# Recurrence of a state-space layer: ACT's and PE's side work moved between slots of a hand-written order

## The chip, the cores and the metric

One core of a Trainium2 chip. The metric is the device time of one execution in microseconds (us), the median of several runs. Engines: PE (matrix products; PEld its weight loads), DVE (vector), ACT (scalar functions), POOL (the general engine, used here for elementwise products), SP (issues DMAs). Each engine takes its own instructions in program order; an instruction that waits holds up all behind it on that engine.

## The reference

Four stages add to x (4 batches of 512 rows, 512 columns): a state-space layer whose gate is x and whose input is a context, a mixture of experts, a cross attention, a ternary feed-forward. The change lies in the first one, which for each batch computes

```
x   = in_proj_w @ hidden_states            (512 channels, 512 times)
u   = silu(conv1d(x, 4 taps) + conv_b)
x_dbl = x_proj_w @ u                       -> dt_lo (16), B (16), C (16)
delta = softplus(dt_proj_w @ dt_lo + dt_proj_b)
state = state * exp(delta * A) + (delta * u) * B     step by step over time
y   = sum over the 16 states of state * C, + D * u
x  += y * silu(layernorm(x))
```

The cross attention later needs keys and values of the same context; their projections are PE work that this kernel puts into the recurrence.

## The kernel before, in words

The recurrence runs over 128 slots: `seq` lists (batch b, chunk c of 128 channels, pair i of states), 4 x 4 x 8. A slot q is one scan over 128 x 1024 elements (two states side by side; a huge delta at the first column resets between them). Eight slots make a chunk, 32 a batch; within a batch the slot is called s. Everything is under a manual schedule: the order in which the Python loop (L658 to L701) calls the steps is the order on each engine.

The main line of slot q:

- POOL: dBu = bb * du for slot q+2 (L491), in three buffers; so it waits for the scan three slots back.
- ACT: dA = exp(delta * negA) for slot q+1 (`decays`, L502), two instructions, into two PSUM buffers; at s = 22 and 28 (`early=True`) those for slots 24 and 30 of the batch are made ahead into SBUF (pool of two buffers, tag dA).
- DVE: the scan (L516). Then hc = h * cb (L517), on POOL in slots 0, 2, 4 of a chunk, else on DVE.
- PE: hc of slot q-1 turned and summed into yT (`sums`, L522), 8 matmuls.
- At slot 2 of a chunk DVE takes the previous chunk's yT (`result`, L556), POOL adds it to x_all (L558).

The next chunk's delta is made meanwhile: PE `dt` at slot 2; ACT `steps_a` at slot 3 (abs, relu, exp: L426 to L428), ACT `steps_ln` at slot 4 (1 + e back into the PSUM bank, L433, and its logarithm, L435); DVE `steps_b` at slot 4, behind the scan (L442 to L444); POOL `step_du` at slot 5 (L452). ACT also makes Du = D * u (`direct`, L540) at slot 3 and evicts the turned gate (L552) at slot 2.

Beside these go three kinds of side work:

- The next batch's input (b < 3): PE `project_in` (L317, s = 1, 6, 11, 16) into PSUM bank "pin"; ACT `take_in` (L321, a slot later) copies it to the one SBUF buffer xin; PE `conv` (L328) one tap in each of the four slots that follow; ACT `take_conv` (L332) at s = 6, 11, 16, 21. Then silu, `project` (s = 23), the rows of B and C (`rows`, L410), which SP stores to DRAM and loads back broadcast, four pairs of 1 MB loads into bb and cb (4 buffers each).
- The values: PE `values` (L473) at odd slots into the one bank "pv"; ACT `take_values` (L479) at the even slot after, to the single buffer v, and SP stores it.
- The keys (L1173 to L1207): PE pk, two slots later ACT's two evictions (L1182, L1183), PE kpss (L1193, also in bank "pv"), and a slot later ACT k_ms (L1205). In batches 0 to 2 five heads each, at s = 6, 14, 22, 26, 30; in batch 3 one at every even slot.

Of the kernel before, what the change touches and what calls it, by code (L numbers as in the profile page):

```python
# [17 lines left out]
F32 = mybir.dt.float32  # L18
# [11 lines left out]
P = 128  # L30
B, S, DM = 4, 512, 512
NT = B * S // P
NC = DM // P
CTX = 256
EPS = 1e-5
DS, DC, DR = 16, 4, 16
NG = 4
# [19 lines left out]
H, HD = 16, 128  # L57
HG = 4
# [182 lines left out]
def ssm_phase(ctx, cm, x_all, w, kv, router_stats):  # L241
# [4 lines left out]
    tc, nc = cm.tc, cm.nc  # L246
    pool = {n: ctx.enter_context(tc.tile_pool(name=f"a_p{n}", bufs=n)) for n in (1, 2, 3, 4, 5)}
    cp = ctx.enter_context(tc.tile_pool(name="a_const", bufs=1))
# [7 lines left out]
    SL = NC * NP  # L256
# [6 lines left out]
    st = {}  # L263

    def load_ctx(b, again=False):

        t = pool[2].tile([P, KC, S], F32, name="ctxb")
        nc.sync.dma_start(t, w["ctxT"][:, b * S:(b + 1) * S].rearrange("(k p) s -> p k s", p=P))
        if again:
            st[b]["ctx"] = t  # L270
            return
        st[b] = dict(ctx=t, u=[], gz=[], delta=[], du=[], bb=[], cb=[],
                     mv=small.tile([P, NC, 2], F32, name="mv"))
# [7 lines left out]
    for n, shape in (("conv_w", [P, NC, DC]), ("conv_b", [P, NC]), ("D", [P, NC])):  # L281
        t = vecs[n] = cp.tile(shape, F32, name=f"v_{n}")
# [18 lines left out]
    bc_dram = dp.tile([B, R // 2, S], F32, name="bc_dram")  # L301

    taps = cp.tile([P, NC, DC, P], F32, name="taps")
    xin = cp.tile([P, S + DC - 1], F32, name="xin")
    nc.vector.memset(xin[:, 0:DC - 1], 0.0)

    def make_taps(c):
        for j in range(DC):
# [4 lines left out]
    def project_in(b, c):  # L313
        s = st[b]
        s["pin"] = ps.tile([P, S], F32, name="pin")
        for k in range(KC):
            nc.tensor.matmul(s["pin"], winT[:, k, c * P:(c + 1) * P], s["ctx"][:, k, :],  # L317
                             start=k == 0, stop=k == KC - 1)

    def take_in(b):  # L320
        nc.scalar.copy(xin[:, DC - 1:], st[b]["pin"])  # L321

    def conv(b, c, j):

        s = st[b]
        if j == 0:
            s["pin"] = ps.tile([P, S], F32, name="pc", tag="pin")
        nc.tensor.matmul(s["pin"], taps[:, c, j, :], xin[:, j:j + S], start=j == 0, stop=j == DC - 1)  # L328

    def take_conv(b, c):  # L330
        u = pool[5].tile([P, S], F32, name="u")
        nc.scalar.activation(u, st[b]["pin"], AF.Identity, bias=vecs["conv_b"][:, c:c + 1])  # L332
        st[b]["u"].append(u)
# [32 lines left out]
    def silu_u(b):  # L366
        for u in st[b]["u"]:
            nc.scalar.activation(u, u, AF.Silu)
        tables(nc)

    def stats(b, c):
        sts = small.tile([P, 6], F32, name="st_a")
        nc.vector.bn_stats(sts, x_all[:, b * NC + c, :])
        nc.vector.bn_aggr(st[b]["mv"][:, c, :], sts)

    def norm(b):
        s = st[b]
        ve = small.tile([P, NC], F32, name="ve_a")
        nc.gpsimd.tensor_scalar(ve, s["mv"][:, :, 1], EPS, None, ALU.add)
        s["rstd"] = small.tile([P, NC], F32, name="rstd_a")  # L380
        nc.gpsimd.tensor_tensor(s["rstd"], ve, half, ALU.pow)
        s["nmr"] = small.tile([P, NC], F32, name="nmr")
        nc.gpsimd.tensor_tensor(s["nmr"], s["mv"][:, :, 0], s["rstd"], ALU.mult)
        nc.gpsimd.tensor_scalar(s["nmr"], s["nmr"], -1.0, None, ALU.mult)

    def silu_gz(b):
        s = st[b]
        for c in range(NC):
            gz = pool[4].tile([P, S], F32, name="gz")
            nc.scalar.activation(gz, x_all[:, b * NC + c, :], AF.Silu, bias=s["nmr"][:, c:c + 1],  # L390
                                 scale=s["rstd"][:, c:c + 1])
            s["gz"].append(gz)
        tables(nc)
# [6 lines left out]
    def take_project(b):  # L400

        xd = st[b]["xd"] = pool[1].tile([R, S], F32, name="xd")
        nc.scalar.activation(xd, st[b]["pd"], AF.Identity, bias=cm.ident[0:R, DR:DR + 1])
        nc.sync.dma_start(bc_dram[b], xd[R // 2:, :])

    def rows(b, g):

        for name, row in (("bb", g * NG), ("cb", DS + g * NG)):
            t = pool[4].tile([P, NG, S], F32, name=name, tag=name)
            nc.sync.dma_start(  # L410
                t, bc_dram[b, row:row + NG, :].unsqueeze(0).to_broadcast([P, NG, S]))
            st[b][name].append(t)
# [62 lines left out]

    def take_values(b, n):
        g, kc = divmod(n, S // P)
        v = pool[1].tile([P, HG * HD], F32, name="v")
        nc.scalar.copy(v, pvs.pop((b, n)))  # L479
        nc.sync.dma_start(kv["v"][b, g, :, kc, :], v)  # L480

# [4 lines left out]
    def inputs(q):  # L486
        if q < len(seq):
            b, c, i = seq[q]
            j = i % 2 * 2
            dBus[q] = pool[3].tile([P, 2, S], F32, name="dBu")  # L490
            nc.gpsimd.tensor_tensor(dBus[q], st[b]["bb"][i // 2][:, j:j + 2, :],  # L491
                                    st[b]["du"][c].unsqueeze(1).to_broadcast([P, 2, S]), ALU.mult)

    def decays(q, early=False):

        if q < len(seq) and q not in dAs:
            b, c, i = seq[q]
            dAs[q] = (pool[2].tile([P, 2, S], F32, name="dA") if early else
                      pda.tile([P, 2, S], F32, name="dA"))
            for j in range(2):  # L500
                n = 2 * i + j
                nc.scalar.activation(dAs[q][:, j, :], st[b]["delta"][c], AF.Exp,  # L502
                                     scale=negA[:, c, n:n + 1])
# [55 lines left out]

    def ahead(b, s):  # L560

        if s in (2, 7, 12, 17):
            take_in(b)
        if s in (6, 11, 16, 21):
            take_conv(b, s // 5 - 1)
        if s in (14, 16, 22, 24):
            stats(b, (14, 16, 22, 24).index(s))
        if s == 20 and b + 1 < B:
            load_ctx(b + 1)
        if s == 20 and b + 1 == B:  # L570
            load_ctx(0, again=True)
        if s == 23:
            silu_u(b)
        if s == 24:
            take_project(b)
        if s == 26:
            norm(b)
        if s == 29:
            silu_gz(b)
        if s in (26, 28, 30, 31):  # L580
            rows(b, (26, 28, 30, 31).index(s))

    def ahead_ends(b, s):

        if s in (22, 28):
            decays((b - 1) * SL + s + 2, early=True)
        if 0 < s < 1 + NC * (1 + DC):
            c, j = divmod(s - 1, 1 + DC)
            project_in(b, c) if j == 0 else conv(b, c, j - 1)
        if s == 23:  # L590
            project(b)

# [9 lines left out]
    def key_at(q, ends, f, *a):  # L602
        key_plan.setdefault((q, ends), []).append((f, a))
# [9 lines left out]
        key_at(q + 3, False, keys.take)  # L613

    for b in range(B - 1):
        for j, (s, bank) in enumerate(((6, "pa"), (14, "pa"), (22, "pin"), (26, "pin"), (30, "pin"))):
            key_at(b * SL + s - 3, False, keys.load, j, j + 1, pool[2], "k_w")
            plan_key(b * SL + s, b + 1, j, bank)
    last_q = (B - 1) * SL
# [5 lines left out]
    def key_steps(q, ends):  # L625
        for f, a in key_plan.pop((q, ends), ()):
            f(*a)
# [29 lines left out]
        rows(0, g)  # L657
    for q, (b, c, i) in enumerate(seq):  # L658
        inputs(q + 2)
        decays(q + 1)  # L660
        key_steps(q, False)
        if i == 2 and q > 2:
            result(*seq[q - 3][:2])
        scan(q)
        if i == 3:
            direct(b, c)
        if q == 0:
            silu_gz(0)
        if q % SL == 8 and b + 1 < B:
            load_x(b + 1)  # L670
        if i == 2:
            take_gate(b, c)

        to = seq[q // NP * NP + NP][0:2] if q + NP < len(seq) else None
        if to is not None:
            if i == 3:
                steps_a(to[0])
            if i == 4:
                steps_ln(to[0])
            if i == 5:  # L680
                step_du(to[0])
        if b + 1 < B:
            ahead(b + 1, q % SL)
        if i == 1:
            gate(b, c)
        if q % 8 == 2 and q + 8 < len(seq):
            load_wv(q // 2 + 4)
        if q % 2:
            values((b + 1) % B, q % SL // 2, wvs[q // 8])
        elif q > 0:  # L690
            take_values(*last)
        last = (b + 1) % B, q % SL // 2
        sums(q - 1)
        if to is not None:
            if i == 2:
                dt(*to)
            if i == 4:
                steps_b(to[0])
        if b + 1 < B:
            ahead_ends(b + 1, q % SL)  # L700
        key_steps(q, True)  # L701
# [1661 lines left out]
```

## Time and profile before

| | us |
|---|---|
| median of 3 runs | 2660.58 (2657.65 to 2661.81) |
| the profiled execution | 2664.86 |
| its span, first to last instruction | 2663.1 |
| recurrence, first to last scan | 34.55 to 534.9 |
| granted PE clock, mean over the span | 0.963 |

In the stretch from 36 to 535 us, instructions of the main line (from the groups of the profile, mean of one):

| | count | us of one |
|---|---|---|
| scan L516, DVE | 128 | 2.35 |
| hc L517, DVE / POOL | 80 / 48 | 1.26 / 2.36 |
| dBu L491, POOL | 127 | 2.38 |
| decays L502, ACT | 252 | 0.70 |
| v L479, ACT | 63 | 0.58 |
| ln L435 / pdt L433, ACT | 15 / 15 | 0.60 / 0.68 |
| steps_b L442 to L444, DVE | 15 each | 0.70, 0.70, 0.69 |

How to read it: an instruction's duration goes to its last write, and the next of the same engine may start some 0.1 us before that, so the spacing of starts is a little under the duration. A bracket at the end of a timeline row gives the idle time of the engine ahead of it and what ended it. Lengths of a chunk, from the first scan of one to that of the next: 32.3, 30.4, 31.4, 33.0 (batch 0); 32.5, 30.9, 29.7, 33.0; 32.6, 31.3, 29.7, 33.0; 34.5, 30.7, 30.7 and the last.

### The profile page before, as it was taken

The numbers are of one execution on the slowest core, as the hardware profiler recorded it, in microseconds if no ns is written. First come the engines' busy times: TensorE is split into PE (matmuls) and PEld (weight loads), VectorE is DVE, ScalarE is ACT, GpSimd is POOL, SyncE is SP. The second block draws the span as 40 slices with busy tenths as digits, with TensorE's granted clock in tenths as the row PEclk, the third lists the DMA queues.
The fourth block names the chain that finished last, engine by engine and source line by source line (L and its number), as shares of the span: only waits on it lengthen the run. The fifth ranks groups of instructions, "written<-read, shape, count | busy, mean of one in ns | idle before, by whom it ended". The sixth has DMA issues, their size and how long they took to land. (4 is left out here: it accounts for less than half of the span.)

```text
span 2663.1 us, 29714 instructions
## 1 busy us (share of the span) xinstructions
PE 2498.2 (94%) x10071; PEld 1411.8 (53%) x10071; DVE 1486.6 (56%) x2551; ACT 1236.5 (46%) x2359; POOL 1183.7 (44%) x1108
## 2 busy tenths in 40 slices
PE   6989898987999999999997999999999999999997
PEld 2555555654565666566664454445555555555543
DVE  6989888855332343344225545456665666555446
ACT  5767676654232222233322444445545555554543
POOL 7899999923233444344426323133422433221112
PEclk8989898988999999999998999999999999999999
DMA  5253535244566767899765543233422433221100
GB/s 199 90 193 114 189 117 182 88 148 152 183 201 198 223 220 246 266 326 324 240 198 167 161 139 107 65 102 124 131 85 90 131 111 107 83 79 61 59 25 20
DMA packets 196143, 395.76 MB, mean 149 GB/s; under 512 B 30340, under 2 KB 71364, under 8 KB 191889
## 3 DMA queue, kind: packets, MB, share of 16 engines
q1 hardware_dynamic: 152926, 238.85, 26.7%
q0 software_dynamic: 41008, 154.76, 18.5%
q8 instruction: 83, 1.36, 0.2%
q10 hardware_dynamic: 2050, 0.18, 0.1%
q14 instruction: 76, 0.61, 0.1%
HBM read 313.88 MB, written 79.82 MB: 148 GB/s over the span
## 5 line engine op out<-in xcount | busy, mean ns | idle before, releaser
L1927 DVE TENSOR_REDUCE mx<-psc 128x1 f32<-128x512 f32 x256 | 176.8, 691 | 461.3 <-PE psc L1924 459.2
L1273 PE MATMUL pg<-xT,wg 128*128 128x284 f32 (+12 forms) x1536 | 403.4, 407 | 1.4 <-ACT xT L1260 1.1
L1273 PEld LDWEIGHTS pg<-xT,wg 128*128 128x128 f32 x1536 | 285.0, 196 | 86.6 <-issue 37.4
L1930 ACT ACTIVATE e<-psc,mx 128x512 f32<-128x512 f32 x256 | 176.1, 688 | 307.1 <-DVE mx L1927 306.8
L491 POOL TENSOR_TENSOR dBu<-bb,du 128x1024 f32<-128x1024 f32 x128 | 302.4, 2378 | 19.4 <-DVE dA L516 17.9
L1214 POOL DMA_INDIRECT xg<-xn_dram,tok x168 | 174.2, 1037 | 214.6 <-PE pt L1257 172.2
L1924 PE MATMUL psc<-kT,qT 128*128 128x512 f32 x512 | 267.3, 604 | 1.0 <-ACT qT L1918 1.0
L1951 PE MATMUL po<-eT,v 128*128 128x512 f32 x512 | 233.1, 598 | 7.5 <-ACT eT L1945 7.1
L1890 PE MATMUL pq<-Wq,xnT 128*128 128x512 f32 x512 | 232.5, 597 | 0.7 <-issue 0.7
L1960 PE MATMUL px<-Wo,oT 128*128 128x512 f32 x512 | 231.8, 596 | 0.0
L502 ACT ACTIVATE dA<-delta,negA 128x512 f32<-128x512 f32 x256 | 177.4, 696 | 109.4 <-DVE hc L517 95.6
L1901 POOL TENSOR_SCALAR qms<-qms 128x4 f32<-128x4 f32 x64 | 25.0, 390 | 412.9 <-DVE qms L1899 412.1
L1944 PEld LDWEIGHTS pet<-ident,e 128*128 128x128 f32 x1024 | 127.9, 142 | 146.4 <-issue 119.9
L516 DVE TENSOR_TENSOR_SCAN dA<-dA,dBu 128x1024 f32<-128x1024 f32 x80 | 187.7, 2347 | 1.9 <-POOL dBu L491 1.9
L1318 DVE COPY yo<-po 128x512 f32<-128x512 f32 x68 | 47.0, 691 | 217.4 <-PE po L1307 217.4
L1951 PEld LDWEIGHTS po<-eT,v 128*128 128x128 f32 x512 | 96.9, 191 | 134.7 <-issue 117.3
L522 PEld LDWEIGHTS yT<-ident,hc 128*128 128x128 f32 x1024 | 121.3, 146 | 81.8 <-issue 37.8
L1814 POOL DMA_INDIRECT yg<-y_dram,pos x124 | 124.9, 1007 | 88.3 <-issue 64.0
L1944 PE MATMUL pet<-ident,e 128*128 128x128 f32 x1024 | 155.2, 274 | 7.7 <-DVE e L1936 7.7
L522 PE MATMUL yT<-ident,hc 128*128 128x128 f32 x1024 | 136.8, 281 | 17.8 <-DVE hc L517 15.1
L1214 POOL DMA_INDIRECT wd<-down,widx x64 | 62.9, 983 | 199.3 <-PE po L1307 178.8
L1945 ACT COPY eT<-pet 128x512 f32<-128x512 f32 x256 | 148.2, 579 | 6.1 <-PE pet L1944 6.1
(355 smaller groups left out, 4405.7 us busy)
## 6 DMA issues: line engine op xcount, KB each, us to landing
y_dram<-yo SPq DMA_DIRECT2D x110, 256.0 KB
bb<-bc_dram SPq DMA_DIRECT2D x16, 1024.0 KB
cb<-bc_dram SPq DMA_DIRECT2D x16, 1024.0 KB
v_dram<-v SPq DMA_DIRECT2D x64, 256.0 KB
k_dram<-k_kT SPq DMA_DIRECT2D x64, 256.0 KB
Wq<-Wq SPq DMA_DIRECT2D x16, 1024.0 KB
kT<-k_dram SPq DMA_DIRECT2D x64, 256.0 KB
rk<-r_dram SPq DMA_DIRECT2D x64, 256.0 KB
```

The costliest lines, as they stand in the source:

```text
L491: nc.gpsimd.tensor_tensor(dBus[q], st[b]["bb"][i // 2][:, j:j + 2, :], st[b]["du"][c].unsqueeze(1).to_broadcast([P, 2, S]), ALU.mult)
L502: nc.scalar.activation(dAs[q][:, j, :], st[b]["delta"][c], AF.Exp, scale=negA[:, c, n:n + 1])
L516: nc.vector.tensor_tensor_scan(*flat, 0.0, ALU.mult, ALU.add)
L522: nc.tensor.matmul(yT[:, lc, :], t[:, lc * P:(lc + 1) * P], cm.ident, is_transpose=True, start=first and lc == 0, stop=last, skip_group_ch ...
L1214: nc.gpsimd.indirect_dma_start(out=t[0:n, :], out_offset=None, in_=table, in_offset=bass.IndirectOffsetOnAxis(ap=index, axis=0))
L1273: nc.tensor.matmul(pg[:, 0:n], s["wg"][:, c, m * P:(m + 1) * P], s["xT"][:, c, 0:n], start=c == 0, stop=c == NC - 1)
L1890: nc.tensor.matmul(pq.rearrange("p h d -> p (h d)"), xnTs[b * NC + i][:, c, :], s["Wq"][:, c, :], start=c == 0, stop=c == NC - 1)
L1924: nc.tensor.matmul(pscore, st[b, g]["qT"][:, h, i * P:(i + 1) * P], ks[n], start=True, stop=True)
L1927: nc.vector.tensor_reduce(mx, pscore, AX.X, ALU.max, negate=True)
L1944: nc.tensor.transpose(pt[:, kc, :], e[:, kc * P:(kc + 1) * P], cm.ident)
L1951: nc.tensor.matmul(po, v[:, kc, :], eT[:, kc, :], start=kc == 0, stop=kc == KB - 1)
L1960: nc.tensor.matmul(px, oTs[j * HG + h][:, i * P:(i + 1) * P], st[b, g]["Wo"][:, h, :], start=h == 0, stop=h == HG - 1)
```

## The change

- `steps_ln` runs at slot 3, straight behind `steps_a`, no longer at slot 4.
- `direct` (Du) runs at slot 1, no longer at 3.
- In batches 0 to 2 `take_values` stands at the head of the even slot, in front of `decays(q + 1)`; v has two buffers. In batch 3 its place is as before.
- `take_in` stands at the slot's end (s = 2, 7, 12, 17), and each chunk takes an xin of its own from the two SBUF buffers of tag dA, with its three leading columns set to zero by DVE. The taps run at s = 3 (the first), 4 (two), 5 (the last), and so on by fives.
- The five key tasks of a batch stand at s = 14, 22, 24, 26, 30.
- The fourth pair of row loads of a batch is issued at s = 1 of that batch itself, no longer at s = 31 of the one before.

The order of instructions on POOL is the same as before; on DVE only the twelve memsets are added.

```diff
-    xin = cp.tile([P, S + DC - 1], F32, name="xin")
-    nc.vector.memset(xin[:, 0:DC - 1], 0.0)
...
     def take_in(b):
-        nc.scalar.copy(xin[:, DC - 1:], st[b]["pin"])
+        t = st[b]["xin"] = pool[2].tile([P, S + DC - 1], F32, name="xin", tag="dA")
+        nc.vector.memset(t[:, 0:DC - 1], 0.0)
+        nc.scalar.copy(t[:, DC - 1:], st[b]["pin"])
...
     def take_values(b, n):
-        v = pool[1].tile([P, HG * HD], F32, name="v")
+        v = pool[2].tile([P, HG * HD], F32, name="v")
...
     def ahead(b, s):
-        if s in (2, 7, 12, 17):
-            take_in(b)
...
-        if s in (26, 28, 30, 31):
-            rows(b, (26, 28, 30, 31).index(s))
+        if s in (26, 28, 30):
+            rows(b, (s - 26) // 2)
     def ahead_ends(b, s):
-        if 0 < s < 1 + NC * (1 + DC):
-            c, j = divmod(s - 1, 1 + DC)
-            project_in(b, c) if j == 0 else conv(b, c, j - 1)
+        if 0 < s < 21:
+            c, j = divmod(s - 1, 5)
+            if j == 0:
+                project_in(b, c)
+            if j == 1:
+                take_in(b)
+            for tap in ((), (), (0,), (1, 2), (3,))[j]:
+                conv(b, c, tap)
...
-        for j, (s, bank) in enumerate(((6, "pa"), (14, "pa"), (22, "pin"), (26, "pin"), (30, "pin"))):
+        for j, (s, bank) in enumerate(((14, "pa"), (22, "pin"), (24, "pin"), (26, "pin"), (30, "pin"))):
...
     for q, (b, c, i) in enumerate(seq):
         inputs(q + 2)
+        ahead_of = b + 1 < B and q % 2 == 0 and q > 0
+        if ahead_of:
+            take_values(*last)
         decays(q + 1)
         key_steps(q, False)
+        if b > 0 and q % SL == 1:
+            rows(b, DS // NG - 1)
...
         scan(q)
-        if i == 3:
+        if i == 1:
             direct(b, c)
...
             if i == 3:
                 steps_a(to[0])
-            if i == 4:
                 steps_ln(to[0])
...
-        elif q > 0:
+        elif q > 0 and not ahead_of:
             take_values(*last)
```

More of the change, by code (lines that the diff above doesn't have):

```diff
@@ L327, in conv @@
             s["pin"] = ps.tile([P, S], F32, name="pc", tag="pin")
-        nc.tensor.matmul(s["pin"], taps[:, c, j, :], xin[:, j:j + S], start=j == 0, stop=j == DC - 1)
+        nc.tensor.matmul(s["pin"], taps[:, c, j, :], s["xin"][:, j:j + S], start=j == 0, stop=j == DC - 1)
     def take_conv(b, c):
```

## The prediction, made before the changed kernel had run

> **What bounds the kernel now.** The change touches only the recurrence, so I first cut the span into windows of about one chunk (eight slots), then read the waits of that stretch, then timelines of single chunks. "Slot" below counts 0 to 7 inside a chunk, "s" counts 0 to 31 inside a batch; batches count from 0.
>
> Windows: length, then busy time of PE, PEld, DVE, ACT, POOL, granted clock, DMA.
>
> ```profile
> 250.00:281.00 31.00, 26.44 (x121) 15.19 (x120) 28.79 (x21) 27.69 (x44) 28.10 (x17) 0.94 0.66 232
> ...
> 316.00:347.00 31.00, 30.86 (x127) 17.48 (x126) 26.95 (x18) 19.47 (x33) 28.61 (x15) 0.95 0.33 102
> ...
> sum 493.00, PE 445.13 PEld 264.07 DVE 432.20 ACT 342.04 POOL 453.53; mean PE 27.82 PEld 16.50 DVE 27.01 ACT 21.38 POOL 28.35
> ```
>
> No engine is full, but POOL (28.35 of 30.8 us per window) and PE are near it, DVE close behind, and the window that prepares the next batch (250 to 281) fills ACT too. The most that closing POOL's holes can give is 493.0 - 453.5 = 39.5 us.
>
> The waits (total, times, longest):
>
> ```profile
> DVE pdt L442 <- ACT ln L435: 37.8, 15, 5.7
> ...
> POOL dBu L491 <- DVE dA L516: 17.9, 16, 2.0
> POOL hc L517 <- DVE hc L516: 17.1, 12, 2.2
> ...
> ACT k_ms L1205 <- PE kpss L1193: 17.3, 13, 2.8
> ACT xin L321 <- PE pin L317: 15.2, 6, 5.0
> ACT v L479 <- DMA v_dram<-v: 6.2, 4, 2.1
> ...
> PE kpss L1193 <- ACT v L479: 18.3, 15, 1.6
> ```
>
> DVE stands 37.8 us for the logarithm, once per chunk; POOL stands 35.0 us for DVE's scans. These are one event: the POOL timeline of batch 2 shows it.
>
> ```profile
> 312.21 2.36 POOL L491 TENSOR_TENSOR dBu<-bb,du 128x1024 f32<-128x1024 f32 x1
> 315.65 2.35 POOL L491 TENSOR_TENSOR dBu<-bb,du 128x1024 f32<-128x1024 f32 x1 [1.08 <-DVE dA L516]
> 319.17 2.37 POOL L491 TENSOR_TENSOR dBu<-bb,du 128x1024 f32<-128x1024 f32 x1 [1.17 <-DVE dA L516]
> 322.70 2.36 POOL L517 TENSOR_TENSOR hc<-hc,cb 128x1024 f32<-128x1024 f32 x1 [1.16 <-DVE hc L516]
> ```
>
> From 283.65 to 314.57 POOL has no hole; DVE stops at slot 4, and two to four slots later POOL has used up its three dBu buffers and waits at the chunk's edge (3.4 us here). So a microsecond taken from DVE's stop is worth a microsecond only until those holes are closed; then POOL's own work is the limit: 8 dBu and 3 hc starting 2.32 apart, 1.23 for x_all, 1.38 for du and its memset, 28.1 us a chunk against 29.7 to 34.5 now.
>
> Why the logarithm is late, in ACT's order of chunk 1, batch 2:
>
> ```profile
> 330.95 0.59 ACT L479 COPY v<-pv 128x512 f32<-128x512 f32 x1 [2.08 <-DMA v_dram<-v]
> 331.44 1.42 ACT L502 ACTIVATE dA<-delta,negA 128x512 f32<-128x512 f32 x2
> 332.79 0.70 ACT L540 ACTIVATE Du<-u,v_D 128x512 f32<-128x512 f32 x1
> ...
> 334.88 0.68 ACT L332 ACTIVATE u<-pc,v_conv_b 128x512 f32<-128x512 f32 x1
> 335.45 1.42 ACT L502 ACTIVATE dA<-delta,negA 128x512 f32<-128x512 f32 x2
> 336.81 0.67 ACT L433 ACTIVATE pdt<-e,ones 128x512 f32<-128x512 f32 x1
> 337.57 0.60 ACT L435 ACTIVATE ln<-pdt 128x512 f32<-128x512 f32 x1
> ```
>
> **Logarithms forward, Du to slot 1.** Nothing is added. Du (0.62 from start to next start), the convolution's take (0.57) and a pair of decays (1.36) no longer stand before ln: 2.55 us earlier, 335.6 instead of 338.17, against scan's end at 335.23. The stop of 2.97 is nearly gone. The decays follow at once and have time: the three delta steps take DVE 2.07 more. Where no take stands between, it is 1.98; the stops are 1.10 to 2.97 in batches 0 to 2, 5.75, 3.33 and 3.68 in batch 3, where a key's eviction (1.05) goes from before ln as well, 3.0 in all. Du in slot 1 lies in a hole of ACT (0.59 to 2.1 before the next decays) and its buffer was read by slot 5's turns; nothing waits.
>
> **Values in front of decays, two buffers.** Removed: the store waits of 6.2, and most of PE's 18.3 for pv's bank, about 1.2 a time (kpss can start after k_sq at 289.8, not 290.89). Added: at even slots ACT's decays stand behind a 0.58 copy that waits for PE's pv matmuls, and behind them the scan of the next slot. At slots 0, 4, 6 the decays have 0.8 to 2.9 us of slack and pv is done. At slot 2 slack is 1.45, and today pv ends at 297.13 against decays that could start at 293.56 (chunk 0), 329.09 against 326.15 (chunk 1), 233.32 against 231.65 (chunk 2): as PE stands, the scan after comes 2.9, 2.2 and 0.95 late. In chunk 0 PE gains 1.2, leaving 1.6. In chunk 1 the pk and kpss of s=6 are gone from PE (1.80 + 0.80), so pv is done first: 0. In chunk 2 all of 0.95 stays; it and the ln gain there (1.10) cancel. The 1.6 of chunk 0 is absorbed, since slot 4 stood 2.97 for dA behind the late input take anyway: that take ended at 301.1, its matmuls move 1.2 forward, v (0.48) is no longer behind it, so scan 4 starts at 301.4, not 303.01, and scan 5 at 306.3, not 309.76: 3.4 us, all of that edge's holes.
>
> **Projection's take at slot's end, own buffer per chunk.** Copies and matmuls are the same in number; of each four taps the first two move one slot later, the last stays, so the convolution's take finds its bank ready as before. Twelve memsets of three columns come onto DVE, 0.06 each (the row of the one there is now): 0.7 in all. The buffers alternate with the early decays, whose readers are two allocations back and done: 0. The memset stands on DVE behind nothing that it waits for.
>
> **One key task from s=6 to s=24.** It moves 2.6 of PE and 1.25 of ACT into the last chunk, the one with ACT at 27.7 of 31. There k_sq's kpss ends near 268.4 by my placement, ln at 271.4, a remaining stop of 0.5 for 1.65; the four gates behind it end 2.3 later (282.2), dA of the last slot at 284.2, where its scan begins now at 284.21. So no gain and no loss there: POOL is without a hole from 258.15 to 283.36 either way.
>
> **Last rows a batch later.** Same two loads of 1 MB. SP now waits for cb's reader at the batch's end, with v, k and Wv transfers queued behind; at slot 1 the buffers are free. First reader is the dBu for slot 6, at 303.9, 14 us after issue; 2.1 MB at the 232 GB/s of a loaded window are 9. Covered by 5 us; without the cover the excess would be a DVE stop. Value 0.
>
> **A rule against it.** The granted clock is 0.5 in pieces of 3.4 us; in one, at 315.7 to 319.1, project_in's four matmuls took 3.64, against 1.88 at full clock. The Trainium skill, TensorE: Matmul & The Clock Gate, section "What's actually happening", says the array falls to half clock after an idle window of about 3.4 us. By the rule, taking 2.6 of PE work from slots 6 to 9 may lengthen that half-clock piece: pv then ends 1.76 later, twice, in front of decays. By the row of today's utilisation there (30.86 of 31) it costs 0. I take 1 us in each of three batches; ends 0 and 3.5.
>
> The 28.1 itself rests on dBu staying at 2.36 while DVE gets denser. The trace has it at that both beside DVE's stop (301.55 to 306.2) and beside its scans; only the scan of s=30, whose dA lies in SBUF, took 3.98 for 2.28 and the du beside it 3.24 for 1.27. That pair stays as it is.
>
> **Sum.** Holes of POOL closed at the two edges 0/1 and 1/2: batch 0 0.94 + 1.16 + 0.97 + 1.17 = 4.2; batch 1 6.1; batch 2 1.08 + 1.17 + 1.16 + 1.96 + 1.16 = 6.5. Batch 3: chunk 0 3.3, then 2.6 and 2.6 with POOL full: 8.5. Together 25.3, less 0.7 and 3.0: 21.6. Routing starts from the last x_all add and its chain is serial, so the end follows. Span 2663.1 - 21.6 = 2641.5 (the profiled run took 2664.9); from the median of 2660.6: **2639**.
>
> **Rivals.** (a) PE does not come forward at slot 2, half of the gain is eaten: 6 to 15 us less time, 2650. For it: PE at 27.8 a window. (b) The stop only changes its releaser: DVE waits for dBu instead of ln, POOL's holes reappear elsewhere: about 2660. Against: DVE's work is 27.7 a chunk, under POOL's 28.1, but only just. (c) Slower: ACT's copy waits for pv at slot 2 at today's PE times, and gate, dt and the exponent chain behind it go late by the same, so ln gains nothing in batches 0 to 2: 2.9 + 2.2 + 0.95 = 6.05, three times 18.2, less batch 3's 8.5: +9.7, 2670. It decides once pv ends over 0.9 us after slot 1's hc in chunks 0 and 1. For it: it does so now by 3.6 and 2.9. Against: kpss and pk leave PE there. (d) All holes close: up to 37 less.
>
> **Chances.** Forecast (15 to 28 less) 0.58, (a) 0.19, (b) 0.08, (c) 0.12, (d) 0.03. About 0.2% (5.3 us) is what a measurement can tell from none. Faster 0.80, same 0.08, slower 0.12. The range runs from 2625, most holes closed, to 2662, within (b).
>
> **What would show it.** DVE's wait for ln under 10 us; POOL's holes at edges 0/1 and 1/2 gone, those of about 2.2 before the hc of s=24 still there; chunk lengths 28 to 29 for chunk 1; ACT v waiting for PE pv 1 to 2 us at slot 2 of chunks 0 and 2. It is wrong if scan 3 of chunks 0 and 1 stands for dA over 2 us and the ln wait stays, or POOL's dBu lengthens over 2.36.

## The result and the profile after

The changed kernel takes 2642.93 us (median of 5 runs, 2637.23 to 2648.25) against 2661.81 for the kernel before in the same comparison, 18.9 less; the ratio is 0.9927, 95% interval 0.9910 to 0.9944. A second comparison on another occasion gave 0.9903 (0.9882 to 0.9924). Forecast were 2639 us and "faster".

The profiled execution is the one of 2642.93 us. Its span is 2641.2, against 2663.1: 21.9 less, where 21.6 were forecast. But these 21.9 are two numbers of opposite sign. From the start of the first scan to the start of the last the recurrence takes 472.24 instead of 498.02, 25.8 less; from there to the end of the span it is 2134.8 instead of 2130.5, 4.3 more, with the same instructions. (What lies ahead of the first scan is 0.45 shorter.) The experiments take up both.

The windows of the changed kernel, a last chunk of a batch, a chunk 1, and nearly all of the recurrence (columns as in the prediction):

```profile
242.00:276.00 34.00, 28.52 (x131) 16.79 (x129) 30.91 (x20) 26.78 (x45) 31.10 (x18) 0.95 0.64 231
305.00:333.00 28.00, 25.27 (x104) 14.08 (x105) 27.07 (x20) 17.62 (x28) 27.65 (x14) 1.00 0.31 99
36.00:506.00 470.00, 429.13 (x1937) 258.51 (x1938) 434.95 (x302) 347.25 (x579) 455.56 (x232) 0.96 0.44 152
```

POOL is now busy 455.56 of 470.0: 14.4 us are left of the 39.5. In the window over a chunk 1 both POOL and DVE are nearly full, 27.65 and 27.07 of 28.0.

The waits of the changed kernel over that last stretch (total, times, longest):

```profile
...
ACT v L480 <- PE pv L474: 47.0, 28, 3.4
...
ACT dA L503 <- DVE hc L518: 31.1, 28, 2.6
...
POOL hc L518 <- DVE hc L517: 8.1, 5, 2.2
...
DVE dA L517 <- ACT dA L503: 6.6, 9, 2.0
...
DVE dA L517 <- POOL x_all L559: 5.9, 3, 2.2
...
DVE pdt L443 <- ACT ln L436: 4.2, 3, 2.6
```

DVE's wait for ln, 37.8 us before, is down to 4.2 (3 times). The first row is new: ACT waits for PE's pv 28 times, 47.0 us. Most of that only replaces ACT's old wait for DVE (95.6 before, 31.1 now). The row of x_all is the part that reached DVE at slot 3 of chunk 2; the scan there waits for dA, which ACT ends 0.1 us ahead of it, and the profile's releaser, an x_all add, is only the event that came last by its count.

POOL at the edge between chunks 0 and 1 of batch 2, where it had three holes of 3.4 us together:

```profile
299.95 7.00 POOL L492 TENSOR_TENSOR dBu<-bb,du 128x1024 f32<-128x1024 f32 x3
307.24 2.35 POOL L518 TENSOR_TENSOR hc<-hc,cb 128x1024 f32<-128x1024 f32 x1 [0.29 <-DVE hc L517]
309.56 4.66 POOL L492 TENSOR_TENSOR dBu<-bb,du 128x1024 f32<-128x1024 f32 x2
```

Three dBu run back to back, and one hole of 0.29 is left. And ACT in chunk 1 of batch 2, from a pair of decays to the logarithm:

```profile
313.51 1.42 ACT L503 ACTIVATE dA<-delta,negA 128x512 f32<-128x512 f32 x2 [0.86 <-DVE hc L517]
316.17 0.60 ACT L427 ACTIVATE e<-pdt 128x512 f32<-128x512 f32 x1 [1.24 <-PE pdt L418]
...
317.80 0.69 ACT L434 ACTIVATE pdt<-e,ones 128x512 f32<-128x512 f32 x1
318.59 0.60 ACT L436 ACTIVATE ln<-pdt 128x512 f32<-128x512 f32 x1
319.08 0.68 ACT L333 ACTIVATE u<-pc,v_conv_b 128x512 f32<-128x512 f32 x1
```

Nothing stands between the exponent and ln any more; ln ends at 319.19 and the scan of slot 4 at the same 319.19, so DVE goes on without a stop (2.97 before).

### The profile page after: what moved, and what is told of

Same layout as the page of the kernel before. It is cut to its first block, busy times and chain, and to the rows that moved or that the text cites. A ratio compares the mean times of both kernels' runs of the same rounds, so it can differ in the third digit from the quotient of the medians.

```text
span 2641.2 us, 29732 instructions
## 1 busy us (share of the span) xinstructions
PE 2474.5 (94%) x10020; PEld 1404.2 (53%) x10071; DVE 1485.0 (56%) x2562; ACT 1237.6 (47%) x2359; POOL 1180.7 (45%) x1108
## 5 line engine op out<-in xcount | busy, mean ns | idle before, releaser
L1953 PEld LDWEIGHTS pet<-ident,e 128*128 128x128 f32 x1024 | 127.9, 142 | 146.3 <-issue 119.9
L503 ACT ACTIVATE dA<-delta,negA 128x512 f32<-128x512 f32 x256 | 176.4, 694 | 52.1 <-DVE hc L518 31.1
```

Of the source, the lines that this page charges most:

```text
L1953: nc.tensor.transpose(pt[:, kc, :], e[:, kc * P:(kc + 1) * P], cm.ident)
```

## The experiments

The experiments weigh two theories. T: the logarithm was DVE's stop, DVE's stop was POOL's holes, and POOL's own work is the limit once they are closed; the values' new place is nearly neutral. R: what pays is the side work, which lets PE come forward. All runs are judged by two numbers: the time against the kernel before, with its interval, and the length of the recurrence, from the start of the first scan to the start of the last, from one profiled execution. The latter is what the change can act on, and it repeats better: the changed kernel was profiled twice and gave 472.2 and 472.9. Single chunks repeat within 0.1 us in batches 1 to 3, but in batch 0 they moved by up to 1.7 (chunk 0: 28.7 and 30.4), so a difference of 1 or 2 us between two kernels is weak evidence. POOL's holes are its idle times of over 0.15 us, without its wait for the first loads of bb (0.5 to 1.0).

| kernel | recurrence, us | POOL's holes in it | ratio to before (95%) |
|---|---|---|---|
| before | 498.0 | 36.3 | |
| the change | 472.2 | 11.9 | 0.9927 (0.9910 to 0.9944) |
| the change again | 472.9 | 11.9 | 0.9903 (0.9882 to 0.9924) |
| logarithm and Du alone | 469.7 | 4.8 | 0.9889 (0.9854 to 0.9925) |
| logarithm alone | 472.2 | 9.2 | one run |
| values in front, buffers alone | 504.7 | 43.3 | 1.0032 (1.0014 to 1.0049) |
| change, values back behind | 472.3 | 9.7 | 0.9895 (0.9870 to 0.9921) |
| change, values behind at slot 2 only | 468.2 | 7.0 | 0.9887 (0.9868 to 0.9906) |
| change, key back at s = 6 | 471.2 | 10.0 | 0.9892 (0.9867 to 0.9918) |
| change, input take in mid-slot | 473.4 | 12.7 | one run |
| change, rows back | 469.9 | 9.3 | one run |
| change, values and take back | 468.8 | 2.1 | 0.9902 (0.9879 to 0.9926) |
| change, hc of slot 4 on DVE | 484.8 | 56.6 | 0.9934 (0.9911 to 0.9957) |

**The logarithm and Du alone.** The kernel before with

```diff
-        if i == 3:
+        if i == 1:
             direct(b, c)
...
                 steps_a(to[0])
-            if i == 4:
                 steps_ln(to[0])
```

> The kernel before with one part alone: logarithm at slot 3, Du at slot 1. Theory T (the logarithm is what DVE stood for, and POOL's holes at the edges between chunks are the same time): DVE's wait for ln falls from 37.8 to under 15 us, the recurrence (first to last scan, 498.0 before, 472.2 after the whole change) comes to 475 to 482, the time falls by 14 to 20. Rival R (the values in front let PE come forward, and that is what pays): the late input take of chunk 0 and the late pv still hold the dA of slot 4, so batches 0 to 2 gain nothing and batch 3 alone its 8.5: recurrence about 489.

Recurrence 469.7: R is out, and T was too cautious (475 to 482). Two moves, the logarithm by one slot and Du by two, shorten the recurrence by 28.3 us, more than the whole change; the intervals of the times overlap. The waits of DVE and POOL in that kernel:

```profile
DVE pdt L442 <- ACT ln L435: 10.2, 11, 2.6
DVE dA L516 <- POOL dBu L491: 4.9, 7, 1.6
DVE hc L516 <- POOL dBu L491: 4.3, 2, 3.9
```

```profile
POOL hc L517 <- DVE hc L516: 4.5, 4, 2.2
```

DVE still stops 10.2 us for ln, but POOL's wait for DVE is down from 35.0 to 4.5: of those stops at most 4.5 still cost anything. POOL has 4.8 us of holes left in 469.7, and DVE now also waits for POOL's dBu (9.2 us, the last two rows of the first list; 5.8 before).

**The logarithm alone**, Du staying at slot 3 in front of it.

> The kernel before with the logarithm at slot 3 alone; Du stays at slot 3 in front of it. T: by the sum of the prediction Du is 0.62 of the 1.98 to 2.55 us by which ln comes earlier; DVE stops 0.6 us longer per chunk than with Du moved (10.2 us in all there), near 20 us in all, and as POOL is full part of it is hidden: recurrence 470 to 478 against 469.7. Rival (Du's place is what matters, since ln's wait is for the bank): above 485.

Recurrence 472.2, in one execution: DVE's wait for ln is 12.0, less than the 20 expected. In part Du then runs where ACT would wait for PE's dt (2.2 us there, 6.6 with Du moved). By these two executions Du's move is worth 2.5 us and ln's 25.8; the 2.5 is too small to be called shown.

**The values in front, alone.** The kernel before with `take_values` at the head of even slots, two v buffers and, for the room, xin from the tag dA, taken in mid-slot as before.

```diff
+        ahead_of = b + 1 < B and q % 2 == 0 and q > 0
+        if ahead_of:
+            take_values(*last)
         decays(q + 1)
```

> The kernel before with the values in front of the decays in batches 0 to 2, two v buffers, and an xin of its own per chunk from the tag dA (which makes the room), taken in mid-slot as before; logarithm, keys and rows as before. T: DVE's wait for ln stays over 30 us, the scan of slot 3 stands for dA by 1 to 3 us in chunks 0 to 2; recurrence 498 to 510, the time the same or up to 12 us longer. R: PE's waits for v go from 18 to under 5 us and the recurrence falls by 10 us or more.

504.7, 6.7 longer than before, and the time 0.3% longer: this part alone is a loss. ACT's wait for pv there, and DVE's waits:

```profile
ACT v L479 <- PE pv L473: 52.1, 33, 4.2
```

```profile
DVE pdt L442 <- ACT ln L435: 41.8, 15, 5.5
DVE dA L516 <- POOL hc L517: 12.6, 3, 4.2
```

The last row is the scan of slot 3 in chunk 2, 4.2 in each of three batches: it starts 6.48 after the scan of slot 2 instead of 2.20. T had put 1 to 3 us in each of chunks 0 to 2; in chunk 0 it was 0 to 1.8, in chunk 1 0.2. ACT's wait for pv is as large as in the changed kernel (47.0), though the pace here is no faster than before. PE's waits for v at kpss did fall, from 18.3 to 7.7, and bought nothing.

**The values back behind**, in the changed kernel (`ahead_of = False`).

> The changed kernel with the values back behind the decays and the rest of the slot in all batches (two v buffers kept). T: ACT's 50 us of waits for pv fall under 10, the scan of slot 3 in chunk 2 starts 1.4 to 2.3 us earlier, PE's waits for v at kpss return; recurrence 466 to 473, so the same time as the changed kernel or up to 6 us less. R: recurrence 480 or more, the time 8 us or more above the changed kernel.

472.3, no different from the change, at the edge of what T gave: chunk 2 falls to 28.5 as expected, but in batches 1 and 2 chunk 0 grows from 28.4 and 28.9 to 30.2 and 30.4, and chunk 1 from 28.6 and 28.2 to 29.5. ACT's wait for pv is nearly gone there (4.1 us, 4 times). So in the company of the other moves the place in front is worth something in chunks 0 and 1 and costs the same in chunk 2.

**Behind at slot 2 only.**

```diff
-        ahead_of = b + 1 < B and q % 2 == 0 and q > 0
+        ahead_of = b + 1 < B and q % 2 == 0 and q > 0 and i != 2
```

> The changed kernel with the values in front of the decays at slots 0, 4 and 6 of a chunk, but at slot 2 behind them as before. T (of what the values' place costs, nearly all lies at slot 2, where the copy waits for pv): the scan of slot 3 in chunk 2 is back at 2.2 us after that of slot 2, chunk 2 falls from 30.0 to 31.5 to 28.5 to 29, and the recurrence from 472.2 to 464 to 469. Rival (what chunk 2 gives back is taken again by a POOL that is full, in chunk 3 and at the next edge): 470 to 473.

468.2, inside T's bounds, the shortest recurrence of all, and with 2633.97 us (2633.41 to 2634.10) the lowest median of those with several runs. What T said of chunk 2 held in batch 0 alone (28.5): in batches 1 and 2 it takes 29.9, and the scan of slot 3 comes 2.94 after that of slot 2, not 2.20, since ACT's copy at slot 0 still waits 3.3 for pv. So slot 2 has part of the cost of the values' place, not nearly all. The interval overlaps that of the change taken on the same occasion (the row "again"), so that it beats the change by more than chance is not shown by the times.

**The key back at s = 6.**

> The changed kernel with the key tasks at s = 6, 14, 22, 26, 30 as before. T: the 2.6 us of PE work come back in front of pv at slots 1 and 2 of chunk 1, so that chunk is 1 to 3 us longer in batches 0 to 2, and chunk 3 loses the 2.0 us that the scan of s = 29 now stands for dA, which POOL hides: recurrence 474 to 482. Rival: the key is the cost in chunk 3 (33.6 us against 33.0 before), and the recurrence is 2 to 6 us shorter than with the change.

471.2: neither range of the total holds. In batches 1 and 2 chunk 1 grows by 1.7 and 2.0 (to 30.3 and 30.15), as T had it, chunk 3 shrinks by 1.3 and 1.6 (to 32.3 and 32.0), and chunk 2 by 1.7 and 0.2: the move is about an even exchange.

**The input take in mid-slot, and the rows a slot earlier**, each undone in the changed kernel.

> The changed kernel with the input take in mid-slot and one tap a slot, as before; the own xin per chunk stays. T: the take in front of the decays of slot 4 was late by PE, not by its place, so nothing changes: recurrence 470 to 475. Rival: the take at slot's end is what freed chunk 0 (32.5 before, 28.4 now), and chunk 0 is 2 us or more longer in each batch: 478 or more.

> The changed kernel with the fourth pair of row loads at s = 31 of the batch before, as before the change. T: covered either way, recurrence 471 to 474. Rival: SP's wait for cb's reader holds the stores behind it, and v's copies wait for them: 2 us or more longer.

473.4 and 469.9, one execution each. Neither part carries the gain. In batches 1 and 2 undoing the take helps chunk 1 (27.7 for 28.2 to 28.6) and chunk 2 (29.7 for 31.5 and 30.0) and costs 0.8 in chunk 3 (34.3 for 33.6); in batch 0 chunk 3 takes 35.9 for 32.0. The rows' move was covered, as expected; the 469.9 is 1.1 below T's bound and 2.4 below the change, most of it in chunk 3 of batch 2 (32.0 for 33.6) and chunk 0 of batch 3 (29.9 for 31.1).

**Both moves undone**, values behind and take in mid-slot; logarithm, Du, buffers, key and rows stay.

> The changed kernel without the two moves that the runs show to be idle or harmful: values behind the decays in all batches, input take in mid-slot; what stays is the logarithm, Du, the two v buffers, xin from dA, the key at 24 and the rows. T: POOL is full and sets the pace, 28.1 a chunk and about 32.5 in chunk 3: recurrence 467 to 472, no faster than the logarithm and Du alone (469.7). Rival: with v's store waits gone (7 us there) it gains 4 us or more over them: under 466.

468.8 with 2.1 us of holes left in POOL, as T has it: next to nothing of POOL's holes is left to close. Logarithm and Du alone reach 469.7 without the second v buffer.

**Is POOL the limit?** In the changed kernel hc of slot 4 goes to DVE.

```diff
-        on_pool = i in (0, 2, 4)
+        on_pool = i in (0, 2)
```

> The changed kernel with hc of slot 4 multiplied on DVE, not on POOL: POOL has 2.32 us less in each chunk, DVE 1.32 more. If POOL now sets the pace and DVE lies just under it (T), DVE takes over at 28.2 to 29.0 a chunk and the recurrence moves little: 474 to 482. If POOL alone sets it and DVE has room, it falls to about 456. If DVE sets it already, it grows by 16 times 1.32 to about 493.

Chunk 1 takes 29.04 in all three batches, chunks 1 and 2 of batch 3 take 28.22 each: just where T put DVE's own work. POOL's waits say the same:

```profile
POOL dBu L492 <- DVE dA L517: 33.6, 28, 2.0
POOL hc L518 <- DVE hc L517: 20.7, 15, 2.2
```

54.3 us of POOL waiting for DVE, for 11.6 in the changed kernel: DVE, with 1.32 us more a chunk, is now the limit. The total of 484.8 lies above T's 474 to 482 because chunk 2 of batches 1 and 2 came to 34.16, with the same 6.48 at slot 2 as in the values-alone kernel. So the two engines are balanced to about 1 us a chunk, and there is no gain in giving this product to DVE; work shifted the other way was not tried. That POOL is the limit with hc of slot 4 on it rests on its holes: 2.1 to 12.7 us in the kernels with the logarithm at slot 3 and this product on POOL.

**The rest of the span.** The changed kernel ran twice under the profiler:

> The changed kernel itself once more, on the same chip as the other kernels of this call. T: recurrence within 2 us of 472.2, and the rest of the span (2134.8 there, 2126 to 2138 in the five kernels so far, though its instructions are the same) follows the half-clock time that PE has outside the recurrence, about 0.3 us for each us of it.

The recurrence repeats (472.9); the rest does not, 2124.9 after 2134.8, from the same instructions. Over the 13 profiled executions the rest runs from 2124.9 to 2138.3, and it goes with the time behind the last scan's start in which PE is granted half its clock (82 to 123 us): 0.31 us for each us, correlation 0.90. An example is the routing and the first experts right behind the recurrence, where by 665 us the change had lost 5.5 of the 26.2 us that it was ahead at the last scan. PE in the kernel before, then in the changed one, in the same instructions:

```profile
600.29 1.05 PE L1193 MATMUL kpss<-ones,k_sq 128*128 128x1 f32 x8 [0.75 <-ACT k_sq L1182]
601.64 0.62 PE L932 MATMUL pc<-map,mT 64*128 64x64 f16 x16 [0.30 <-DVE map L922]
```

```profile
576.63 1.87 PE L1202 MATMUL kpss<-ones,k_sq 128*128 128x1 f32 x8 [0.74 <-ACT k_sq L1191]
578.43 1.03 PE L941 MATMUL pc<-map,mT 64*128 64x64 f16 x16
```

In the changed kernel a half-clock stretch lies over them (573.9 to 584.2 by the clock record), in the one before it begins at 602.4, behind them. Between the two executions of the changed kernel the rest differs by 9.9 us, so this change does not fix it. That it is chance alone was not tested, nor that the half clock is the cause: it is a correlation.

## Why the prediction was right, and where it was not

**What bounds the kernel** held: DVE's stop for ln and POOL's holes were one event, and POOL is the limit behind it. The first experiment shows both: with the logarithm and Du moved and nothing else, DVE's wait for ln fell by 27.6 us, the recurrence by 28.3, and POOL was left with 4.8 us of holes. The exchange of hc shows DVE to be close behind.

**The sum.** Holes closed were put at 25.3 us; the recurrence became 25.8 shorter. By batch, forecast 4.2, 6.1, 6.5, 8.5; measured 7.1 (127.0 to 119.9), 4.1 (126.2 to 122.0), 6.0 (126.7 to 120.6), 8.5 (118.2 to 109.7). Batch 3, which of the moves has the logarithm, Du, the rows and v's second buffer, comes out at its 8.5, from 9.1 gained in chunks 0 to 2 and 0.6 lost in the last. The total is right partly by luck: the errors of batches 0 and 1, +2.9 and -2.0, nearly cancel. The floor that the sum rests on held: dBu takes 2.39 on the mean (2.38 before), and chunk 1 28.2 to 28.6, for the 28.1 of POOL's own work.

**The two deductions**, 3.7 us together, were wrong, and it is luck that the 4.3 us of the rest, which the prediction put at nothing, took their place: without it the span would have been 26 us shorter, and against the second execution it is 30.7. The memsets cost DVE nothing that shows (0.7 were taken): the one at slot 2 starts inside the result's tail, and the scan behind still comes 0.60 after the result, as before. The half-clock deduction of 3 us had the wrong sign. In slots 6 to 9, for which it was made, batches 1 and 2 had one piece of 3.4 us each before and have none now, and none with the key put back at s = 6 either, so the work taken from PE did no harm. Up to the last scan PE's half-clock time fell from 88.7 to 47.8 us. It is 88.7 as well with the values in front alone, and 37.5 to 61.4 in the eleven executions with the logarithm moved: it goes with the logarithm's place. Nor is the idle window of about 3.4 us in the rule of the Trainium skill (TensorE: Matmul & The Clock Gate, "What's actually happening") what the trace before shows ahead of the piece that the prediction quotes:

```profile
313.42 1.09 PE L522 MATMUL yT<-ident,hc 128*128 128x128 f32 x8 [0.88 <-DVE hc L517]
315.48 3.64 PE L317 MATMUL pin<-ctxb,winT 128*128 128x512 f32 x4 [0.96 <-ACT u L332]
```

PE's longest pause there was 0.96, and none exceeded 2.5 in the 10 us ahead of any half-clock piece that begins in the recurrence.

**Values in front of decays** was where the working failed. "At slots 0, 4, 6 the decays have 0.8 to 2.9 us of slack and pv is done" is not so in the trace before either. At slot 0 of chunk 1, batch 2:

```profile
320.46 1.42 ACT L502 ACTIVATE dA<-delta,negA 128x512 f32<-128x512 f32 x2 [0.72 <-DVE hc L517]
...
320.71 1.88 PE L473 MATMUL pv<-Wv,ctxb 128*128 128x512 f32 x4
```

The decays began at 320.46, the scan that they feed at 322.53, and pv ended at 322.59. The values-alone kernel bears it out at the old pace: ACT waited 33 times, 21 of them at slots 0, 4 and 6. The changed kernel waited 28 times, not about twice a batch. At some slots the new pace adds to it. At s = 16 of batches 1 and 2 pv ended 2.4 us before the decays began; with the logarithm and Du moved alone it ends 0.2 after, chunks 0 to 2 giving PE 1 to 4 us less while its work is the same. In total the pace is not what makes ACT wait: 52.1 us at the old one, 47.0 at the new, and 4.1 with the copy back behind. Chunk 2 of batch 2 of the changed kernel shows how the wait at slot 0 grows into that of slot 2:

```profile
333.23 0.59 ACT L480 COPY v<-pv 128x512 f32<-128x512 f32 x1 [2.90 <-PE pv L474]
333.71 1.42 ACT L503 ACTIVATE dA<-delta,negA 128x512 f32<-128x512 f32 x2
...
336.11 0.69 ACT L333 ACTIVATE u<-pc,v_conv_b 128x512 f32<-128x512 f32 x1
...
341.90 0.59 ACT L480 COPY v<-pv 128x512 f32<-128x512 f32 x1 [0.99 <-PE pv L474]
342.39 1.42 ACT L503 ACTIVATE dA<-delta,negA 128x512 f32<-128x512 f32 x2
```

The copy at slot 0 waits 2.90; the convolution's take (u) behind it comes late by that. PE's project_in waits 1.05 for u and starts at 336.85, kpss and pv stand behind it, pv ends at 341.87, and ACT's copy at slot 2 waits for that pv. In place of the 0.95 forecast the scan after slot 2 came 1.5 (batch 2) to 2.3 us late (batch 1). On DVE, chunk 2 of batch 1:

```profile
218.75 2.28 DVE L517 TENSOR_TENSOR_SCAN hc<-dA,dBu 128x1024 f32<-128x1024 f32 x1
223.26 2.30 DVE L517 TENSOR_TENSOR_SCAN dA<-dA,dBu 128x1024 f32<-128x1024 f32 x1 [2.23 <-POOL x_all L559]
```

So chunk 2 became longer in batches 1 and 2 (29.7 to 31.5 and 30.0), not equal. The 3.4 us of chunk 0 that I explained through the values and PE coming forward did come (32.5 to 28.4, 32.6 to 28.9), but the logarithm and Du alone give 28.9 and 28.6 there: that explanation was not needed. Rival (c) was right that the copy waits for pv at slot 2, 30.5 us over batches 0 to 2 of the values-alone kernel. Its sizes were not: the scan after slot 2 came 1.7 to 1.8 late in chunk 0 of batches 1 and 2, 0.2 in chunk 1 and 4.3 in chunk 2, for 2.9, 2.2 and 0.95, and that recurrence grew by 6.7, not 18.2. It was beaten because the logarithm's gain does not depend on the values.

**The key** was to cost nothing; chunk 3 became 0.5 longer in batches 1 and 2 (33.0 to 33.6), against 1.3 to 2.0 saved in chunk 1. The stop at slot 4 there, put at 0.5 for 1.65, was 2.0, and not for ln: ACT's copy at the head of s = 28 waited 2.16 for pv with the decays behind it, in batch 2:

```profile
381.27 0.58 ACT L480 COPY v<-pv 128x512 f32<-128x512 f32 x1 [2.16 <-PE pv L474]
381.75 1.42 ACT L503 ACTIVATE dA<-delta,negA 128x512 f32<-128x512 f32 x2
```

With the key back at s = 6 that wait is 0.2 in batch 1 and 0.6 in batch 2. Yet chunk 3 takes 33.8 and 33.5 with the logarithm and Du alone too, so its length has more than this one cause; they were not taken apart.

**The end follows** held to within the scatter of the rest, which is a sixth of the gain in this execution (4.3 of 25.8) and two fifths of it between two executions of one kernel (9.9). No sum over the recurrence could have known that scatter.

## What to carry to other kernels

When a fast engine stops once per period and a full one has a hole some slots later, they are one loss: find the one instruction that the stop waits for, count what stands ahead of it on its own engine, and move that; here the logarithm's move did nearly all of the work. A copy that waits for another engine does not belong in front of the instructions that feed the main line: that it hardly ever waited at the end of its slot (once, 1.5 us, before) says nothing of the head. Compare, slot by slot, when its input ends with when the copy would start, and allow for the new pace, since an engine whose work per period does not shrink (PE here) comes later against the others. Try the parts of a bundle alone: of six moves the logarithm paid 25.8 us, Du perhaps 2.5 (one run), the values cost 6.7 alone and nothing in company, the key and the input's take exchanged time between chunks, and the rows were covered.

## What the runs showed of the hardware

The same 2130 us of program took 2124.9 to 2138.3, in step with PE's half-clock time. Such stretches last multiples of 3.4 us in the clock record of the changed kernel (3.4 to 17.1), and in one of them eight kpss matmuls took 1.87 in place of 1.05. In the recurrence before they came without a long idle of PE: no pause in the 10 us ahead of one exceeded 2.5 us. Where they fall behind the recurrence differs between executions, so a comparison of two spans sees up to 10 us (2134.8 and 2124.9 for one kernel) that the length of the changed part itself does not have (472.2 and 472.9).
